# A two-layer graph kernel: the gathers of a tile issued in three parts, with a one-element GpSimd copy between them, and another order at the ends of blocks

## The chip, the core and the metric

The kernel runs on one core of a Trainium2 chip. The core has five engines that run their own instruction streams and meet only at semaphores: TensorE (PE in the profile, with its weight loads as PEld), VectorE (DVE), ScalarE (ACT), GpSimd (POOL) and SyncE (SP). Sixteen DMA engines move data between the device's memory and the on-chip memory. DMAs that take their row numbers from a list, gathers and scatters, are issued by GpSimd, which spends time on each. The metric is the device time of one execution in microseconds (us); the number to beat is the median of 12 runs.

## The reference

There are 4096 nodes with 128 features each, and an adjacency matrix of 4096 x 4096 in which about 0.8% of the entries are one, so that a node has some 32 neighbours. Two layers follow one another:

```
# layer 0: attention with 8 heads
Wh  = x @ W[h]                          # 8 heads, 128 features
e   = leaky_relu(f1[i] + f2[j], 0.2)    # f1 = Wh.a1, f2 = Wh.a2
att = softmax(e over the neighbours j of i)
h   = elu(att @ Wh);  x1 = layernorm(x + elu(concat(h) @ W1 + b1)) * gamma + beta
# layer 1: quantiles over the neighbours
keep  = neighbours of i without every m-th one (m from the number of neighbours)
agg   = mean of the 25%, 50% and 75% quantiles of x1[j], j in keep, per feature
out   = (0.5 * agg + 0.5 * x1) @ Wl.T + bl + x1
```

## The kernel before

The work goes through three stages. First, the adjacency matrix is read (ACTq line 820) and turned into lists: for each row VectorE finds the positions of the ones with maximum and replace instructions (`neighbours`, lines 811 to 870, a generator that works in small pieces). The rows of a block are then ranked by the number of their neighbours (`complete_records`, `rank_by_count`; the result is the tile `ranks`, line 998), and GpSimd scatters their records in that order to device memory (`rec_d`, line 354). There are five blocks of 4, 6, 8, 8 and 6 tiles, 128 rows each: 32 tiles in all.

Second comes the attention, tile by tile. SyncE loads the sorted records of a tile and its short lists (`load_rows`, lines 1037 to 1062). VectorE transposes them into lists of row numbers (`list_rows`: `idx`, `f1b`, `f1x`). GpSimd gathers the neighbours' rows from `xt_d` into the buffer `G` or `Gs`, 128 rows by one DMA (`fetch_rows`, through `gather`, line 345). A tile takes 27 to 49 gathers, 1152 in all. The weighing (`weigh_rows`) then works on what has landed: VectorE adds the scores (`z`, lines 1133 and 1134), ScalarE takes the exponential (line 1135), VectorE spreads it into weights (`pf`, line 1160; first half, then second half), TensorE multiplies them with the gathered rows (`y`, line 1188), ScalarE copies the product out (`raw`, line 1201), and VectorE divides by the sums: `rden` (lines 1208 and 1209), then `raw` (line 1211). Every four tiles or so, `transform` makes the layer's output from them, and its rows are scattered to `x_d` (the names `x1_d` of the source stand without digits in the profile).

Third, the quantiles: GpSimd gathers each node's kept neighbours from `x_d` (`vals`), and VectorE sorts them by comparisons (lines 1462 and 1464).

The order in the second stage is written out by hand, in one loop over tiles (lines 583 to 626). In the turn of tile k, the loop issues all gathers of tile k, and after each three of them one waiting scatter (`put_one`, line 571). Then `work(k - 1)` weighs the tile in front, whose gathers were issued in the turn before. Between the steps of the weighing stand pieces of the next block's lists (`behind`, an equal share of them, `each`, after each step), and the preparing of the next tile's row lists (`soon`). In the turn before a block's last tile, the share holds the completing and the ranking of the next block too. In the turn of the block's last tile (`end`), the scatters of the next block's records (`place(b + 1)`) go between the first gathers, and SyncE's loads of the next two tiles are issued after them. `G` has two buffers, `pf` four, `rden` two.

```
weigh.append(fetch_rows(tc, pools, ready.pop(k), xt_d, uses, put_one, k == NT - 1))
while aside:
    put_one()
if end and b < final:
    load(k + 1)
    load(k + 2)
work(k - 1, behind, left, soon)
```

Of the kernel before, what the change touches and what calls it, by code (L numbers as in the profile page):

```python
# [24 lines left out]
P = 128  # L25
# [63 lines left out]
LMAX = 2 * max(HT)  # L89
ROOM = max(2 * HT[u[0]] * len(u) for u in UNITS)  # L90
TURN = 12
EARLY = []


# [274 lines left out]
def kernel(  # L369
# [97 lines left out]

    rp = tc.alloc_tile_pool(name="recp", bufs=1)
    rec = rp.tile([P, NT, REC], F32, name="rec")
    num = rp.tile([P, NT], F32, name="num")  # L470
    oneb = rp.tile([P, P], BF16, name="oneb")
    before = rp.tile([P, P], BF16, name="before")
# [60 lines left out]
        t = sum(BLOCKS[:b]) + i  # L533
        ready[k] = list_rows(tc, pools, *loaded.pop(k), t, bad)

    def work(k, behind, quota, soon=None):

        def more():
            nonlocal quota
            if quota:  # L540
                quota -= 1
                next(behind, None)

        if k >= 0:
            R, parts = weigh.pop(0)
            at = len(members)
            members.append(R)
            each = -(-quota // (len(parts) + 9))
            for turn, _ in enumerate(
                weigh_rows(tc, attp, pp, parts, turned, at, consts, k == NT - 1)  # L550
            ):
                if soon and turn == len(parts):
                    soon()
                    soon = None
                if tails and next(tails[0], True):
                    tails.pop(0)
                for _ in range(each):
                    more()
            if len(members) == size[k]:
                tails.append(  # L560
                    transform(tc, attp, pp, kp, turned.pop(0), list(members), consts, store)
                )
                members.clear()
        if soon:
            soon()
        while quota:
            more()

    aside = []

    def put_one():
        if aside:
            scatter(nc, *aside.pop(0))

    for _ in prepare(0):
        pass
# [5 lines left out]
    with tc.manual_schedule(engines=ALL):  # L582
        for k, (b, i) in enumerate(seq):
            n = BLOCKS[b]
            end = i == n - 1
            behind, left = None, 0
            if b < final:
                if i == 0:
                    nxt = prepare(b + 1)
                    todo = BLOCKS[b + 1] * PIECES + -(-BLOCKS[b + 1] // 8) + 1  # L590
                if not end:
                    behind, left = nxt, -(-todo // (n - 1 - i))
                    todo -= left
            elif i == 0:

                cp.release()
                adjp.release()
                wp = tc.alloc_tile_pool(name="order", bufs=1, side="right")
                cp = tc.alloc_tile_pool(name="cnt_all", bufs=2, side="right", reuse_waits="tile")
                found = rank_by_count(tc, cp, kp, num, jp1, before, oneb, 0, NT)  # L600
                order = wp.tile([P, NT], I32, name="order")
                nc.vector.tensor_copy(order, found)
                cp.release()
                cp = tc.alloc_tile_pool(name="lists", bufs=2, side="right", reuse_waits="tile")
                pools.append(cp)
                waiting = list(range(NT))
            if not end:
                if i + 2 < n:
                    load(k + 2)
            soon = (lambda: prep(k + 1)) if not end else None  # L610
            aside.extend((x1_d, *args) for args in store)
            store.clear()
            if end and b < final:
                aside.extend(place(b + 1))
            if b == final:
                aside.extend((all_d, rec[:, t, 0:REC1], order[:, t : t + 1]) for t in waiting[:3])
                waiting = waiting[3:]
            weigh.append(fetch_rows(tc, pools, ready.pop(k), xt_d, uses, put_one, k == NT - 1))
            while aside:
                put_one()  # L620
            if end and b < final:
                load(k + 1)
                load(k + 2)
            work(k - 1, behind, left, soon)
            if end and b < final:
                prep(k + 1)
        for t in waiting:
            scatter(nc, all_d, rec[:, t, 0:REC1], order[:, t : t + 1])
        R = wp.tile([P, NT, REC1], F32, name="all")
        idx = wp.tile([P, NT, L], I32, name="idx")  # L630
        nc.sync.dma_start(R, all_d.rearrange("(t p) w -> p t w", p=P))
        work(NT - 1, None, 0)
        rows = kept_rows(tc, wp, R, jp1, pidx, idx, own_i, bad, limits, (0, 24, 16, 8))
        for left in range(64):
            if left == 2:
                next(rows)
            if tails and next(tails[0], True):
                tails.pop(0)
        assert not tails
        for args in store:  # L640
            scatter(nc, x1_d, *args)
        nc.vector.tensor_scalar(lane, lane, 31, None, ALU.bitwise_and)
        nc.vector.tensor_copy(lanef, lane)
        for t, parts in enumerate(every):
            for w, g in capacity(parts)[1]:
                wider = cp.tile([P, 1], F32, name="wider")
                nc.vector.tensor_scalar(wider, lanef, float(g), float(w), ALU.is_ge, ALU.mult)
                nc.vector.tensor_tensor(holds[:, t : t + 1], holds[:, t : t + 1], wider, ALU.add)
        nc.vector.tensor_tensor(bad[:, 4, :], bad[:, 4, :], holds, ALU.is_gt)
        count_bad(tc, cp, kp, bad, ones, total)  # L650
# [222 lines left out]
def complete_records(tc, cp, rec, num_all, bad, jp1, pidx, t0, n):  # L873
# [3 lines left out]
    for a in range(t0, t0 + n, step):  # L877
# [28 lines left out]
        for i, s in enumerate((sk, sk2)):  # L906
# [15 lines left out]
        nc.vector.tensor_scalar(keys, keys, -1.0, float(N), ALU.mult, ALU.add)  # L922
        nc.vector.tensor_tensor(rec.bitcast(I32)[:, a : a + m, 0:L], keys, pads, ALU.add)
        nc.vector.tensor_copy(rec[:, a : a + m, R_NUM], num)
        nc.gpsimd.iota(
            rec.bitcast(I32)[:, a : a + m, R_OWN],
            pattern=[[P, m]],
            base=a * P,
            channel_multiplier=1,
        )  # L930
        yield


# [161 lines left out]
def fetch_rows(tc, ap, lists, xt_d, turn, between, halves):  # L1095


    nc = tc.nc
    R, todo = lists
    parts = []  # L1100
    G, room = None, 0
    done = 0
    for at, (s0, w, g0, idx, f1v) in enumerate(todo):
        k = P // w
        if w - g0 > room:
            rest = 0
            for _, v, h0, _, _ in todo[at:]:
                if rest + v - h0 > 32:
                    break
                rest += v - h0  # L1110
            room = 18 if at and rest <= 18 else 32
            G, col = take(ap, [P, room, XW], "Gs" if room == 18 else "G", turn), 0
        parts.append((w, k, g0, G[:, col : col + w - g0, :], f1v))
        col += w - g0
        room -= w - g0
    for half in (0.5, 1) if halves else (1,):
        for (w, _, g0, G, _), (_, _, _, idx, _) in zip(parts, todo):
            for g in range(max(g0, int((half - 0.5) * w) if halves else 0), int(half * w)):
                gather(nc, G[:, g - g0, :], xt_d, idx[:, g : g + 1])
                done += 1  # L1120
                if done % 3 == 0:
                    between()
    return R, parts


def weigh_rows(tc, ap, pp, parts, turned, place, consts, halves):


    nc = tc.nc
# [17 lines left out]
    for half in range(2):  # L1147
        pfs = []
        for (w, k, g0, G, f1v), z in zip(parts, zs):
            g2 = w // 2  # L1150
            a = max(g0 - half * g2, 0)
            if a >= g2:
                pfs.append(None)
                continue
            if halves:
                here = slice(half * g2 + a - g0, (half + 1) * g2 - g0)
                scores(z[:, here], G[:, here, D + 1 :], f1v[:, here])
            pf = ap.tile([P, H * P // 2], F32, name="pf", bufs=4)
            spread = [P, g2 - a, k, H]
            nc.vector.tensor_tensor(  # L1160
                pf.rearrange("p (g k h) -> p g k h", g=g2, k=k)[:, a:],
                z[:, half * g2 + a - g0 : (half + 1) * g2 - g0, :].unsqueeze(2).to_broadcast(spread),
                own[w].unsqueeze(1).unsqueeze(3).to_broadcast(spread),
                ALU.mult,
            )
            pfs.append(pf)
        yield
        for b in range(4):
            if b % 2 == 0:
# [37 lines left out]
    rden = ap.tile([P, H], F32, name="rden")  # L1207
    nc.vector.tensor_scalar(rden, raw[:, :, D], TINY, None, ALU.max)
    nc.vector.reciprocal(rden, rden)
    yn = raw[:, :, 0:D]  # L1210
    nc.vector.tensor_tensor(yn, yn, rden.unsqueeze(2).to_broadcast([P, H, D]), ALU.mult)  # L1211
    yield
# [478 lines left out]
```

## Time and profile before

| what | value |
|---|---|
| median of 12 runs | 3515.74 us (3509.89 to 3520.33) |
| profiled execution | 3511.04 us |
| its span in the trace | 3509.0 us |
| busy share: DVE, POOL, ACT, PE | 75%, 65%, 36%, 22% |
| gathers of the attention: number, mean of one on GpSimd | 1004 into G, 1002 ns; 148 into Gs, 991 ns |
| gathers of the quantiles: number, mean of one | 1028, 946 ns |

The profile is of one execution; its span is 2 us shorter than that execution's time, and that is 4.7 us under the median. Busy shares are means over stages with different limits. Times inside the trace are counted from the span's start. "issue" as a releaser is time in which the engine waited for nothing that the profile shows. POOL lines of gathers and scatters show GpSimd's own part of the DMA, not the transfer.

### The profile page before, as it was taken

What the parts mean: (1) busy time and instruction counts of PE and PEld (TensorE: products, weight loads), DVE (VectorE), ACT (ScalarE), POOL (GpSimd) and SP (SyncE); (2) the same over time, 40 slices, a digit from 0 to 9 for tenths busy, and PEclk for the clock granted to TensorE, in tenths of its full rate; (3) what the DMA queues carried; (4) which work ended last, traced back from release to release, by engine and by line L of the source; (5) the groups of instructions that cost most, each with busy time, mean ns of one, the idle gap of its engine ahead of it and who ended that gap; (6) DMA issues with size and microseconds to landing.
All of it is one profiled execution on the core that took longest, in us unless ns stands there. A gap on an engine that the chain in (4) does not pass through costs nothing. (4 is left out here: it accounts for less than half of the span.)

```text
span 3509.0 us, 17209 instructions
## 1 busy us (share of the span) xinstructions
PE 758.3 (22%) x2717; PEld 439.2 (13%) x2717; DVE 2625.7 (75%) x4737; ACT 1253.1 (36%) x1843; POOL 2293.2 (65%) x2450
## 2 busy tenths in 40 slices
PE   1113524333243434234411000011000000000001
PEld 1011211211112111111300000000000000000001
DVE  7694875657545554313257999999999999999998
ACT  3132332233122312112213444444444544444443
POOL 0477777777777777777647777773575576667530
PEclk9956756666576656567655555555555555555555
DMA  5543442433333322222112122210111111112100
GB/s 186 128 135 98 126 127 68 121 107 108 78 87 107 91 55 60 59 52 52 44 39 53 53 52 53 53 52 26 37 48 38 37 49 43 43 44 52 42 22 4
DMA packets 118646, 239.35 MB, mean 68 GB/s; under 512 B 55744, under 2 KB 72128, under 8 KB 110336
## 3 DMA queue, kind: packets, MB, share of 16 engines
q0 software_dynamic: 75392, 159.16, 18.2%
q10 hardware_dynamic: 12160, 68.49, 5.7%
q1 hardware_dynamic: 30976, 10.53, 1.6%
q14 instruction: 93, 0.76, 0.1%
q8 instruction: 25, 0.41, 0.1%
HBM read 226.82 MB, written 11.18 MB: 68 GB/s over the span
## 5 line engine op out<-in xcount | busy, mean ns | idle before, releaser
L1464 DVE TENSOR_TENSOR vals<-low,vals 128x1024 f32<-128x1024 f32 (+9 forms) x1342 | 1581.3, 1215 | 64.5 <-DMA vals<-x_d,idx 22.5
L345 POOL DMA_INDIRECT vals<-x_d,idx x1028 | 972.8, 946 | 557.0 <-issue 305.7
L345 POOL DMA_INDIRECT G<-xt_d,idx x1004 | 1005.7, 1002 | 310.5 <-issue 301.7
L1462 ACT COPY low<-vals 128x1024 f32<-128x1024 f32 (+6 forms) x739 | 725.8, 984 | 917.7 <-DVE vals L1464 870.3
L1188 PE MATMUL y<-G,pf 128*64 128x258 f32 (+1 forms) x1072 | 244.6, 522 | 656.9 <-DVE pf L1160 488.4
L715 PE MATMUL fin<-share,vals 128*128 128x128 f32 x294 | 70.9, 420 | 1302.1 <-DVE vals L1464 1097.8
L1201 ACT COPY raw<-y 32x258 f32<-32x258 f32 (+1 forms) x480 | 175.0, 365 | 335.6 <-PE y L1188 331.1
L1133 DVE TENSOR_TENSOR z<-G,f1x 128x256 f32<-128x256 f32 (+6 forms) x43 | 20.4, 475 | 324.2 <-DMA G<-xt_d,idx 319.7
L715 PEld LDWEIGHTS fin<-share,vals 128*128 128x128 f32 x294 | 63.8, 317 | 1309.0 <-DVE vals L1464 1026.5
L1135 ACT ACTIVATE z<-z 128x256 f32<-128x256 f32 (+8 forms) x77 | 22.9, 302 | 548.7 <-DVE z L1134 536.0
L1188 PEld LDWEIGHTS y<-G,pf 128*64 128x64 f32 (+1 forms) x1072 | 119.5, 189 | 771.7 <-DVE pf L1160 539.7
L854 DVE MAX8 first<-sgn 128x8 f32<-128x128 bf16 x1024 | 211.9, 277 | 2.0
L345 POOL DMA_INDIRECT Gs<-xt_d,idx x148 | 146.7, 991 | 45.1 <-issue 41.8
L826 ACT ACTIVATE sgn<-adj_t 128x2048 bf16<-128x2048 int32 x64 | 122.0, 1906 | 113.1 <-DVE first L854 96.8
L1188 PE MATMUL y<-Gs,pf 128*128 128x258 f32 (+1 forms) x364 | 136.1, 485 | 0.0
L1220 ACT COPY yT<-turned 128x512 f32<-128x512 f32 x64 | 65.2, 1019 | 169.7 <-PE turned L1219 169.7
L866 DVE MAX8 rec<-first 128x8 f32<-128x256 f32 x256 | 108.8, 425 | 7.1
L354 POOL DMA_INDIRECT rec_d<-rec,ranks x32 | 33.3, 1041 | 120.1 <-DVE ranks L998 101.4
L1160 DVE TENSOR_TENSOR pf<-z,own 128x512 f32<-128x512 f32 (+2 forms) x134 | 80.2, 636 | 32.8 <-ACT z L1135 18.3
L354 POOL DMA_INDIRECT out_dram<-o,own_i x32 | 31.7, 992 | 101.1 <-ACT o L745 83.8
L1248 PE MATMUL o<-hv,W_sb 128*128 128x512 f32 (+2 forms) x160 | 80.9, 612 | 70.7 <-DVE hv L1242 70.6
L1219 PE MATMUL turned<-ident,raw 128*128 128x128 f32 x256 | 62.4, 390 | 153.6 <-DVE raw L1211 98.7
(185 smaller groups left out, 1486.5 us busy)
## 6 DMA issues: line engine op xcount, KB each, us to landing
adj_t<-in_adj_dram ACTq DMA_DIRECT2D x64, 1024.0 KB
vals<-x_d,idx POOLq DMA_INDIRECT x1028, 2.5
G<-xt_d,idx POOLq DMA_INDIRECT x1004, 2.6
R<-rec_d SPq DMA_DIRECT2D x128, 26.4 KB
score<-rec_d SPq DMA_DIRECT2D x184, 1.0 KB
Gs<-xt_d,idx POOLq DMA_INDIRECT x148, 2.6
xt_d<-rec SPq DMA_DIRECT2D x4, 548.0 KB
rec<-in_x_dram SPq DMA_DIRECT2D x4, 512.0 KB
```

Of the source, the lines that this page charges most:

```text
L345: nc.gpsimd.indirect_dma_start(out=dst, out_offset=None, in_=rows, in_offset=bass.IndirectOffsetOnAxis(ap=idx, axis=0),)
L715: nc.tensor.matmul(fin[:, i, :], lhsT=v, rhs=w, start=(a == 0), stop=(a == len(terms) - 1), skip_group_check=True,)
L826: nc.scalar.activation(sgn, adj_t, AF.Sign, accum_out=cnt[:, i : i + 1])
L854: nc.vector.max(first[:, ts(c0 // CW + c, 8)], key[:, b * (512 // CW) + c, :])
L866: nc.vector.max(top, first)
L1160: nc.vector.tensor_tensor(pf.rearrange("p (g k h) -> p g k h", g=g2, k=k)[:, a:], z[:, half * g2 + a - g0 : (half + 1) * g2 - g0, :].unsqu ...
L1188: nc.tensor.matmul(yv[p0 : p0 + m], lhsT=pf, rhs=rhs, start=not any(over[:i]), stop=not any(over[i + 1 :]), skip_group_check=True,)
L1201: nc.scalar.copy(raw[p0 : p0 + m, 4 * half + b - 1 : 4 * half + b + 1, :], y[p0 : p0 + m, :, a : a + D + 1],)
L1220: nc.scalar.copy(yT[:, :, ts(place, P)].rearrange("p h (u g) -> p g u h", u=4)[:, ts(half, 16)], t_ps.rearrange("p b (g u h) -> p (b g) u ...
L1248: nc.tensor.matmul(o, lhsT=consts["W1_sb"][:, h, :], rhs=hv[:, ts(j, n)], start=(h == 0), stop=(h == H - 1),)
L1462: nc.scalar.copy(kept, low)
L1464: nc.vector.tensor_tensor(high if end else low, kept, high, ALU.max if end else ALU.min)
```

## The change

Six edits, of which the first three make one whole:

- `fetch_rows` no longer issues the gathers. It returns a generator that stops before the 11th and before the 26th gather of the tile (`FOLLOW = (10, 25)`).
- The loop issues the first ten gathers of tile k and then calls `work(k - 1)`. When the weighing of tile k - 1 has written its first `pf`, GpSimd copies one element of that `pf` to a 1 x 1 tile `follow`, and issues the gathers up to the 25th. When the weighing has written `rden`, GpSimd copies one element of it and issues the rest. The first and the last tile's gathers are issued in one go, as before. This makes 61 copies: 31 of `pf`, 30 of `rden`, each behind a wait for VectorE.
- Since a later write to a `pf` or `rden` buffer has to wait for the copy that reads it, VectorE gets waits for GpSimd, 30 more than before.
- In the turn before a block's last tile, the completing and the ranking of the next block (`held`) come after the whole weighing, and no more between its steps. The share `each` is counted without them.
- In the turn of a block's last tile, the scatters of the next block's records start after 15 gathers in place of 3 (`later` lets four turns of `put_one` pass). SyncE's loads of the next two tiles still come behind them.
- The numbers of the own rows (`iota` into `rec`, line 925), written per block by five GpSimd instructions of which four stand between gathers, are written once at the start for all tiles.

The instructions of SyncE keep their order. On ScalarE and TensorE a few instructions of the turns before a block's last tile change places with VectorE's.

```diff
+FOLLOW = (10, 25)
...
+nc.gpsimd.iota(
+    rec.bitcast(I32)[:, :, R_OWN], pattern=[[P, NT]], base=0, channel_multiplier=1
+)
...
-    def work(k, behind, quota, soon=None):
+    def work(k, behind, quota, soon=None, held=0, issue=None, go_on=None):
...
-            if quota:
+            if quota > held:
...
-            each = -(-quota // (len(parts) + 9))
+            each = -(-(quota - held) // (len(parts) + 9))
+            seen = []
...
+                if issue and seen:
+                    nc.gpsimd.tensor_copy(follow, seen.pop()[0:1, 0:1])
+                    if next(issue, True):
+                        issue = None
+                        go_on()
...
     def put_one():
         if aside:
             scatter(nc, *aside.pop(0))
+        elif later:
+            if later[0]:
+                later[0] -= 1
+            else:
+                scatter(nc, *later[1].pop(0))
+                if not later[1]:
+                    later.clear()
...
+                    held = 0 if todo else -(-BLOCKS[b + 1] // 8) + 1
...
-                aside.extend(place(b + 1))
+                later.extend((4, place(b + 1)))
...
-            weigh.append(fetch_rows(tc, pools, ready.pop(k), xt_d, uses, put_one, k == NT - 1))
-            while aside:
-                put_one()
-            if end and b < final:
-                load(k + 1)
-                load(k + 2)
-            work(k - 1, behind, left, soon)
+            fetched, issue = fetch_rows(tc, pools, ready.pop(k), xt_d, uses, put_one, k == NT - 1)
+            weigh.append(fetched)
+            def go_on():
+                while aside or later:
+                    put_one()
+                if end and b < final:
+                    load(k + 1)
+                    load(k + 2)
+            if k == 0 or k == NT - 1:
+                for _ in issue:
+                    pass
+            else:
+                next(issue)
+            work(k - 1, behind, left, soon, held, issue, go_on)
...
-        nc.gpsimd.iota(
-            rec.bitcast(I32)[:, a : a + m, R_OWN], ...
-        )
...
+    def issue():
+        done = 0
+        for half in (0.5, 1) if halves else (1,):
+            for (w, _, g0, G, _), (_, _, _, idx, _) in zip(parts, todo):
+                for g in range(...):
+                    if done in FOLLOW:
+                        yield
+                    gather(nc, G[:, g - g0, :], xt_d, idx[:, g : g + 1])
+                    done += 1
+                    if done % 3 == 0:
+                        between()
...
+        if half == 0:
+            seen.append(pfs[0])
         yield
...
     nc.vector.reciprocal(rden, rden)
+    seen.append(rden)
```

More of the change, by code (lines that the diff above doesn't have):

```diff
@@ L547, in work @@
             members.append(R)
-            each = -(-quota // (len(parts) + 9))
+            each = -(-(quota - held) // (len(parts) + 9))
+            seen = []
             for turn, _ in enumerate(
-                weigh_rows(tc, attp, pp, parts, turned, at, consts, k == NT - 1)
+                weigh_rows(tc, attp, pp, parts, turned, at, consts, k == NT - 1, seen)
             ):
+                if issue and seen:
[3 more added lines that the diff above has]
+                        go_on()
                 if soon and turn == len(parts):
@@ L563, in work @@
                 members.clear()
+        if issue:
+            for _ in issue:
+                pass
+            go_on()
         if soon:
             soon()
+        held = 0
         while quota:
             more()
-    aside = []
+    follow = const.tile([1, 1], F32, name="follow")
+    aside, later = [], []
     def put_one():
@@ L585 @@
             end = i == n - 1
-            behind, left = None, 0
+            behind, left, held = None, 0, 0
             if b < final:
@@ L617 @@
                 waiting = waiting[3:]
-            weigh.append(fetch_rows(tc, pools, ready.pop(k), xt_d, uses, put_one, k == NT - 1))
-            while aside:
-                put_one()
-            if end and b < final:
-                load(k + 1)
-                load(k + 2)
-            work(k - 1, behind, left, soon)
+            fetched, issue = fetch_rows(tc, pools, ready.pop(k), xt_d, uses, put_one, k == NT - 1)
[7 more added lines that the diff above has]
+            if k == 0 or k == NT - 1:
+                for _ in issue:
+                    pass
+            else:
+                next(issue)
+            work(k - 1, behind, left, soon, held, issue, go_on)
             if end and b < final:
@@ L924, in complete_records @@
         nc.vector.tensor_copy(rec[:, a : a + m, R_NUM], num)
[L925 to L929, printed above, removed]
-        )
         yield
@@ L1101, in fetch_rows @@
     G, room = None, 0
-    done = 0
     for at, (s0, w, g0, idx, f1v) in enumerate(todo):
@@ L1115, in fetch_rows, with weigh_rows @@
         room -= w - g0
[L1116 to L1126, printed above, removed]
+    def issue():
+        done = 0
+        for half in (0.5, 1) if halves else (1,):
+            for (w, _, g0, G, _), (_, _, _, idx, _) in zip(parts, todo):
+                for g in range(max(g0, int((half - 0.5) * w) if halves else 0), int(half * w)):
+                    if done in FOLLOW:
[4 more added lines that the diff above has]
+                        between()
+    return (R, parts), issue()
+def weigh_rows(tc, ap, pp, parts, turned, place, consts, halves, seen):
     nc = tc.nc
```

## The prediction

> **What bounds the kernel now.** I read the page first: its engine lines and the slices, to see which engine is full in which stage.
>
> ```profile
> PE 758.3 (22%) x2717; PEld 439.2 (13%) x2717; DVE 2625.7 (75%) x4737; ACT 1253.1 (36%) x1843; POOL 2293.2 (65%) x2450
> ...
> DVE  7694875657545554313257999999999999999998
> POOL 0477777777777777777647777773575576667530
> ```
>
> A slice is 87.7 us. From slice 21 on VectorE is at 9 of 10: the quantile stage is VectorE's. In slices 3 to 20 VectorE falls to 5 and less while GpSimd stands at an even 7. The chain of waits that ended last is no help (it ends in the last scatter at once), so I asked for busy time by stage, cut where GpSimd issues its first and its last gather of the attention:
>
> ```profile
> core 0: us, PE busy (x) PEld busy (x) DVE busy (x) ACT busy (x) POOL busy (x), PEclk, DMA share, GB/s
> 126.00:1732.00 1606.00, 573.95 (x1993) 283.90 (x1993) 888.98 (x2821) 423.86 (x814) 1229.45 (x1231) 0.65 0.34 90
> ```
>
> GpSimd is busy for 1229 of 1606 us, and the waits in that window say where the other 376 are:
>
> ```profile
> POOL G L345 <- issue: 301.7, 992, 0.3
> POOL Gs L345 <- issue: 41.8, 137, 0.3
> POOL rec_d L354 <- issue: 11.4, 28, 2.2
> ...
> POOL G L345 <- DVE f1b L1082: 5.4, 1, 5.4
> ```
>
> Nearly all of it is 0.3 us before each of some 1230 DMAs, which nothing outside GpSimd causes. Its stream is one DMA after another at 1.25 to 1.3 us, and no row says that a gather waited for TensorE to free G. So this stage is GpSimd's stream, end to end, and whatever is put into it moves the end one for one: the 73 us of scatters and tails behind it and the 1704 us of quantiles follow in order. VectorE, at 889 of 1606 us, is late only where GpSimd is made to wait for it, and that is what the change does.
>
> **A copy between two gathers.** The trace of before has no GpSimd copy, but it has four small GpSimd operations between gathers, the iotas of line 925. Here is one in the timeline (start, duration, idle time before it in brackets):
>
> ```profile
> 956.89 0.94 POOL L345 DMA_INDIRECT Gs<-xt_d,idx  x1 [0.30 <-issue]
> 957.85 0.16 POOL L925 IOTA rec<- 128x8 int32 x1
> 958.16 0.95 POOL L345 DMA_INDIRECT G<-xt_d,idx  x1 [0.15 <-issue]
> 959.42 0.94 POOL L345 DMA_INDIRECT G<-xt_d,idx  x1 [0.30 <-issue]
> ```
>
> From the end of one gather to the start of the next are 957.83 to 958.16 = 0.33 us in place of 0.30: the iota lies in the 0.3 us that GpSimd needs anyway. A copy whose wait is over costs 0.02 us if it is like that. From above I bound it by 0.3 us: about the longest small operation of the start, where the affine select over 128x128 takes 0.28, with none of it hidden. I take 0.05, near the iota, which is the nearest row in place and size. For 61 copies: 3 us, ends 1 and 18. Two rows of this case plead for the upper part: a copy reads on-chip memory where the iota only writes, and gathers, which read their list there, show a mean of 1002 ns where most take 944. That is (1002 - 944) x 1004 + (991 - 944) x 148 = 65 us of lengthening over the stage, 0.06 us for each, and they lengthen mostly while VectorE runs operations with two tiles as inputs.
>
> The Trainium skill, SBUF — State Buffer, section "Who interferes with whom", says more sharply that a VectorE instruction with two SBUF inputs and a GpSimd one that reads SBUF exclude each other, whichever starts second being held for the whole of the other. By that rule, taken for the stalled copies below, each `rden` copy would be held by line 1211, the division right behind `rden`; with 1.2 us from the trace's row for it, four stalls would cost an estimated 5 us more, and the sum below would be 18. The trace has no GpSimd compute instruction beside line 1211 to show it, and my sum leaves it out.
>
> **The waits.** A wait costs what is left of the weighing of tile k - 1 when GpSimd arrives. For each turn I set the end of the first `pf` and of `rden` of tile k - 1 against the end of the 10th and of the 25th gather of tile k, all read from the timelines. The first `pf` ends 2 to 12 us after the turn's first gather starts, the 10th gather 12 to 20: no `pf` copy waits; the smallest margin is 1.2 us (turn 14). `rden` ends at 17 to 54, the 25th gather at 32 to 43. It is late in six turns: 1 by 2.7, 2 by 21.5, 5 by 6.1, 10 by 0.8, 14 by 2.8, 16 by 12.6 us. Turn 5, for one:
>
> ```profile
> 367.22 0.94 POOL L345 DMA_INDIRECT G<-xt_d,idx  x1 [0.30 <-issue]
> ...
> 400.05 0.94 POOL L345 DMA_INDIRECT G<-xt_d,idx  x1 [0.30 <-issue]
> ...
> 406.88 0.20 DVE L1209 RECIPROCAL rden<-rden 128x8 f32<-128x8 f32 x1
> ```
>
> The first row is the turn's first gather, the second its 25th, done at 400.99; `rden` is done at 407.08.
>
> Turns 2 and 16 are turns before a block's last tile, and the new order mends them. In turn 2 completing and ranking run on VectorE from 37.7 to 53.8 us and `rden` directly after; with `held` behind the weighing, and two pieces after a step in place of three, `rden` comes at about 30, before the 25th gather at 32.6. In turn 16 they run from 21.9 to 40.5; without them, and with one piece for two, `rden` comes at about 27 against 32.8. So both cost nothing; if that cover failed they would cost the 34 us above. The other four remain: 2.7 + 6.1 + 0.8 + 2.8 = 12.4 us. After a release GpSimd starts 0.26 us later (a scatter released at 1780.40 starts at 1780.66), then the copy at 0.16 and 0.15 to the next gather: 0.57 in place of 0.3, so four times 0.27 = 1.1 us more. Behind the waiting copy stand the tile's remaining gathers, then the next tile's; VectorE, ScalarE and TensorE wait for those, so the delay isn't won back.
>
> **The block ends.** The scatters of line 354 come 12 gathers, 15 us, later. At the end of block 0 GpSimd waited for `ranks` before:
>
> ```profile
> 266.22 1.67 POOL L354 DMA_INDIRECT rec_d<-rec,ranks  x1 [2.25 <-issue]
> ...
> 272.92 1.01 POOL L354 DMA_INDIRECT rec_d<-rec,ranks  x1 [1.24 <-issue]
> ```
>
> (`ranks` ended at 265.4.) Both go: 2.25 + 1.24 - 2 x 0.3 = 2.9 us. What is late next is the row lists: SyncE loads after the last scatter has landed, and the first `idx` of the next tile was there 9.1 to 9.4 us after that scatter was issued (blocks 0 to 2; all three lists after 15). The last scatter was at 33 to 41 us of a last turn of 70 to 74; at 45 to 56 it leaves the first `idx` at 55 to 66, still 7 us or more before the next tile's first gather. VectorE idles 15 us longer for the records there, off the path. The four iotas that leave the stream give 0.1 us, and the one at the start lies in the 101 us that GpSimd waits for the first `ranks`. SyncE's queue keeps its order.
>
> VectorE's new waits: a tile with five or more `pf` writes its fifth into the buffer that the copy reads, so it waits for GpSimd's 10th gather. Before, that write came at 9.9 us in turn 27 and the 10th gather ended at 17.0, at most 7 us late, in turns where `rden` has 12 to 21 us to spare. Nothing.
>
> **The sum.** 12.4 + 1.1 + 3 - 2.9 - 0.1 = +13.5 us on the profiled execution's 3511.0, so 3524.5; the median of the runs is 4.7 higher, which makes 3529. A measurement of this kernel can tell about 0.2% (7 us) from no change.
>
> **The rivals.** *Faster, by spacing out.* If pauses and the later scatters keep gathers out of VectorE's two-input operations, the 65 us of lengthening shrink. From a quarter of it on the sign turns: 16 of 65 pay the 13.5. Half of it gives -19, 3497. For it: the lengthened gathers come in runs beside VectorE work. Against: 55 and more of 61 copies find their wait over, so the gathers keep their places. *No difference.* The four late turns are paced by VectorE's pieces, and a delay of GpSimd in one gives VectorE air for the rest; then the waits vanish and +1 - 3 leaves about -2 to +4: 3514 to 3520. Against: VectorE waits for the gathers at the start of each weighing (320 us in total), so it starts the next one late by as much. *Slower, by a chain of waits.* If the weighing slips by 5 us against the gathers, turns with less margin join (4, 6, 8, 13, 22 and 24 have 1.0 to 4.7): 12 us from them and 20 from the four, +45, 3561. That the copies don't hold GpSimd at all is excluded: each carries a wait for VectorE, and the gathers behind it are in the same stream.
>
> **How the numbers follow.** The forecast (+5 to +30) has 0.55, the chain 0.12, no difference 0.13, faster by spacing 0.20. Of the forecast's share 0.05 lies under +7. So faster 0.20, same 0.18, slower 0.62. The forecast's own range is 3518 to 3546. For 8 in 10 I go down to 3504, which takes in no difference and the weak half of spacing out, and up to 3548: copies at their upper end with the four waits are 12.4 + 1.1 + 18 - 3 = +28.5, 3544, and a little of the chain.
>
> **What would show it.** Right: copies at 0.1 to 0.2 us in some 0.3 us of gap; GpSimd's waits for `rden` in turns 1, 5, 10 and 14 and 12 us in all; none for `pf`; the two waits for `ranks` gone; the last attention gather some 13 us later; gathers' means at 1002 and 991. Wrong: a mean of G gathers under 985 (spacing out); `rden` waits in ten or more turns (chain); none at all (no difference); a gather waiting for `idx` at a block's end, for which I have priced nothing.

## The result, and the profile after

The changed kernel takes 3551.4 us (median of 7 runs, 3545.8 to 3554.5) against 3515.7 before (28 runs): a ratio of 1.0101, 95% interval 1.0091 to 1.0110, so 32 to 39 us slower. Its profiled execution spans 3547.8 us, 38.8 more than the one before. On another occasion the same kernel took 3550.3 against 3513.3, ratio 1.0105 (1.0090 to 1.0121). The profiled execution of before lies 4.7 us under its median and this one 1.8, so the difference between the profiled executions is some 3 us larger than that of the medians.

I read the same views again. The engine lines of the page, and the stretch from the first to the last gather of the attention:

```profile
PE 753.9 (21%) x2717; PEld 438.0 (12%) x2717; DVE 2624.9 (74%) x4737; ACT 1253.3 (35%) x1843; POOL 2314.4 (65%) x2507
```

```profile
core 0: us, PE busy (x) PEld busy (x) DVE busy (x) ACT busy (x) POOL busy (x), PEclk, DMA share, GB/s
125.90:1770.20 1644.30, 567.89 (x1991) 282.19 (x1991) 886.98 (x2817) 423.81 (x813) 1250.32 (x1287) 0.65 0.33 88
```

The stretch is 1644 us long where it was 1605 (the window of before above ends 0.7 us behind its last gather), and that is the whole difference: what lies ahead of the first and behind the last gather is unchanged. VectorE has nearly the same work in it, 887 us where it was 889. GpSimd is busy 21 us more, and idle 18 us more; these are rows of its waits, from the start to 1850 us:

```profile
POOL follow L558 <- DVE rden L1243: 14.9, 4, 7.5
...
POOL all_d L355 <- issue: 12.8, 18, 7.8
...
POOL rec_d L355 <- issue: 8.5, 28, 0.3
...
POOL follow L558 <- DVE pf L1192: 6.5, 2, 4.9
```

The columns are total, number and longest. Four copies wait for `rden` and two for `pf`. The first scatter into all_d, which had 0.3 us ahead of it, now has 7.8. The two waits for `ranks` at the end of block 0 are gone (28 scatters at 0.3 each). And this is the price of the copies themselves, from the view by groups (x count, busy, mean ns, idle before):

```profile
L558 POOL COPY follow<-rden 1x1 f32<-1x1 f32 x30 | 10.2, 340 | 15.0 <-DVE rden L1243 14.9
L558 POOL COPY follow<-pf 1x1 f32<-1x1 f32 x31 | 9.8, 318 | 6.6 <-DVE pf L1192 6.5
```

For the 60 copies inside the stretch: 19.9 us of busy time, and 9.5 us in place of 18.3 from them to the next DMA, so 11.1 us net. The stream's books close: waits for `rden` 14.9, for `pf` 6.5, the copies 11.1, the scatter into all_d 7.5, the waits for `ranks` -2.9, and 1.9 from all that remains (G gathers at a mean of 1005 ns, Gs at 975), together 39.

### The profile page after: what moved, and what is told of

Same layout as the page of the kernel before. It is cut to its first block, busy times and chain, and to the rows that moved or that the text cites. A ratio compares the mean times of both kernels' runs of the same rounds, so it can differ in the third digit from the quotient of the medians.

```text
span 3547.8 us, 17318 instructions
## 1 busy us (share of the span) xinstructions
PE 753.9 (21%) x2717; PEld 438.0 (12%) x2717; DVE 2624.9 (74%) x4737; ACT 1253.3 (35%) x1843; POOL 2314.4 (65%) x2507
## 5 line engine op out<-in xcount | busy, mean ns | idle before, releaser
L346 POOL DMA_INDIRECT G<-xt_d,idx x1004 | 1009.0, 1005 | 302.4 <-issue 286.1
L1167 ACT ACTIVATE z<-z 128x256 f32<-128x256 f32 (+8 forms) x77 | 23.0, 302 | 645.7 <-DVE z L1166 645.3
L1192 DVE TENSOR_TENSOR pf<-z,own 128x512 f32<-128x512 f32 (+2 forms) x134 | 80.2, 635 | 37.9 <-POOL follow L558 21.5
L1095 DVE COPY bad<-R 128x1 f32<-128x1 f32 x32 | 4.7, 148 | 132.3 <-DMA R<-rec_d 132.3
```

The lines of the kernel that those rows point to most:

```text
L346: nc.gpsimd.indirect_dma_start(out=dst, out_offset=None, in_=rows, in_offset=bass.IndirectOffsetOnAxis(ap=idx, axis=0),)
L1192: nc.vector.tensor_tensor(pf.rearrange("p (g k h) -> p g k h", g=g2, k=k)[:, a:], z[:, half * g2 + a - g0 : (half + 1) * g2 - g0, :].unsqu ...
```

## Where the waits come from: the block ends

Turn 5 looks as predicted, only longer: the first row is the turn's 25th gather, the others what GpSimd and VectorE do about the copy.

```profile
402.84 0.94 POOL L346 DMA_INDIRECT G<-xt_d,idx  x1 [0.30 <-issue]
411.24 1.17 POOL L558 COPY follow<-rden 1x1 f32<-1x1 f32 x1 [7.46 <-DVE rden L1243]
```

```profile
410.90 0.20 DVE L1243 RECIPROCAL rden<-rden 128x8 f32<-128x8 f32 x1
411.14 1.23 DVE L1246 TENSOR_TENSOR raw<-raw,rden 128x1024 f32<-128x1024 f32 x1
```

The copy is released with `rden`, comes to lie beside the division of line 1246, and takes 1.17 us. The four copies that waited for `rden` all took 1.16 or 1.17.

The waits for `pf` stand in turns 5 and 10, 1.6 and 4.9 us. Turn 10 is the first turn behind the end of block 1 (turn 5 is the second behind that of block 0), and the reason stands in VectorE's timeline before it:

```profile
598.63 0.17 DVE L1242 TENSOR_SCALAR rden<-raw 128x8 f32<-128x8 f32 x1 [2.11 <-ACT raw L1235]
...
635.51 0.15 DVE L1095 COPY bad<-R 128x1 f32<-128x1 f32 x1 [34.02 <-DMA R<-rec_d]
...
645.53 0.45 DVE L1114 STREAM_TRANSPOSE f1x<-f1b 128x256 f32<-128x256 f32 x1
645.90 0.60 DVE L1165 TENSOR_TENSOR z<-G,f1x 128x256 f32<-128x256 f32 x1
```

The same place in the trace of before, where turn 10 began at 633.0:

```profile
607.03 0.15 DVE L1068 COPY bad<-R 128x1 f32<-128x1 f32 x1 [17.30 <-DMA R<-rec_d]
...
616.89 0.45 DVE L1087 STREAM_TRANSPOSE f1x<-f1b 128x256 f32<-128x256 f32 x1
617.26 0.60 DVE L1133 TENSOR_TENSOR z<-G,f1x 128x256 f32<-128x256 f32 x1
```

VectorE waits 34 us for the records of the next block, where it waited 17; over the stage its waits for them are 132.3 us in six, where they were 70.2. Turn 10 begins at 645.7. Before, the lists (`f1x` is the last of them) were complete 16 us ahead of that turn and VectorE had begun the weighing (`z`) by then; now they are complete as it starts. So the first `pf` ends at 18.5 us of the turn, not at 10, and `rden` at 43.5, not at 35.5.

The same at the last block's end. There VectorE has, behind the lists, the ranking of all 32 tiles, which ends with `order`; the scatters into all_d need it:

```profile
1463.08 0.18 DVE L626 COPY order<-ranks 128x32 int32<-128x32 int32 x1
1463.45 0.60 DVE L1165 TENSOR_TENSOR z<-G,f1x 128x256 f32<-128x256 f32 x1 [0.19 <-issue]
1464.03 1.00 POOL L355 DMA_INDIRECT all_d<-rec,order  x1 [7.80 <-issue]
```

The same in the trace of before:

```profile
1415.78 0.18 DVE L602 COPY order<-ranks 128x32 int32<-128x32 int32 x1
...
1424.92 1.00 POOL L354 DMA_INDIRECT all_d<-rec,order  x1 [0.30 <-issue]
```

`order` was complete at 1416.0 there and the first of these scatters was issued at 1424.9, so it waited for nothing. In the changed kernel the wait is labelled "issue", but the scatter reads `order`, and starts 0.8 us after its end.

That gives the theory: the late block ends cost the 7.5 us, all of the `pf` waits and part of the `rden` waits; the copies cost 11 us, because VectorE's two-input operations hold them; what is left are the four late turns that the prediction priced. The rival: the copies and their waits make all of it.

## Experiments

**The scatters where they were.** Copies and `held` stay.

```diff
-                later.extend((4, place(b + 1)))
+                later.extend((0, place(b + 1)))
```

> The copies and `held` stay; the next block's records are scattered again right behind the third gather of a block's last tile. Theory (late records): the scatters that come 15 us later keep VectorE idle for the records (132.3 us in 6 waits against 70.2 before), so that the next block's lists, the weighing and `order` stand 15 us later in its queue. Then this run loses the 7.8 us wait ahead of the first scatter into all_d in turn 26 and both `pf` waits (6.5 us), its `rden` waits fall from 14.9 to about 12, near the 12.4 of the prediction, and the waits for `ranks` at the end of block 0 come back (2.9 us): 38.9 - 7.5 - 6.5 - 2.5 + 2.9 = +25 us over before, some 3541. Rival (the copies by themselves): the `pf` waits and the late `order` come from VectorE being held by copies and waits earlier in the stream, the ends have no part in it, and only the 2.9 come back: +42 us, some 3557, with all_d still waiting 7 us or more.

Measured: 3536.7 us against 3516.5, ratio 1.0058 (1.0043 to 1.0074), so +20 us (15 to 26), where the theory expected 25 and the rival 42; the profiled execution, 3537.5, has a stretch of 1630.2 us, 25 more than before. GpSimd's waits:

```profile
POOL rec_d L355 <- DVE ranks L1025: 104.0, 2, 101.3
...
POOL follow L558 <- DVE rden L1243: 11.2, 4, 5.0
...
POOL all_d L355 <- issue: 5.7, 19, 0.3
```

No wait for `pf`, none ahead of all_d, a wait of 2.8 us for `ranks` back, and the `rden` waits at 1.5, 5.0, 1.5 and 3.4 us in turns 1, 5, 10 and 14. That is the theory, and the 11.2 us stand close to the prediction's 12.4, which were worked out for these ends. Some 15 of the 36 us between the medians belong to the later scatters.

**The new order without copies.** All gathers of a tile in one go; `held` and the later scatters stay.

```diff
-            if k == 0 or k == NT - 1:
-                for _ in issue:
-                    pass
-            else:
-                next(issue)
-            work(k - 1, behind, left, soon, held, issue, go_on)
+            for _ in issue:
+                pass
+            go_on()
+            work(k - 1, behind, left, soon, held)
```

> The new order at the block ends (`held`, scatters 12 gathers later) stays; the gathers of a tile are issued in one go and there is no copy. Theory: what is left is the late `order` in turn 26 (+7.5 us) and the gone waits for `ranks` (-2.9): +3 to +7 us, 3519 to 3523, with VectorE's waits for the records still near 130 us in 6, and no wait of GpSimd for `pf` or `rden`. Rival (the order alone makes the weighing late enough to stop the gathers, by G buffers that come free too late): +15 us or more, with waits of G for TensorE or VectorE in the stream. Second rival (`order` is late only because the copies delayed VectorE): -3 us, 3513, and no wait ahead of the first scatter into all_d.

Measured: 3516.6 against 3516.5, ratio 1.0002 (0.9993 to 1.0011). The late `order` is there without any copy, which rules out the second rival:

```profile
POOL all_d L355 <- issue: 13.3, 19, 7.8
```

VectorE's waits for the records are 128.3 us in six, and no gather waits for a buffer. But the time came in lower than expected: the interval ends at +4 us. The stretch of the profiled execution is 4.5 us longer than before, at which the books stand (7.5 - 2.9), while the medians are equal: the profiled execution of before lies 4.7 us under its median, this one 0.4. So whether the 5 us are paid isn't settled; by itself the new order costs 4 us at most. It becomes dear with copies, since only they make GpSimd wait for the late weighing of turns 5 and 10.

**Copies that need not wait.** 61 copies at the same places, of a constant.

```diff
-                    nc.gpsimd.tensor_copy(follow, seen.pop()[0:1, 0:1])
+                    seen.pop()
+                    nc.gpsimd.tensor_copy(follow, ones[0:1, 0:1])
```

> 61 copies at the same places in the stream, of one element of a constant that was written at the start, in place of `pf` and `rden`: they read as before but wait for nothing. Theory (a copy costs by what VectorE does beside it): the copies still come to a mean of some 250 to 320 ns, since most of them meet VectorE's two-input operations by chance, the four that stood right beside line 1246 lose their 1.17 us; all 21.4 us of waits are gone, and the late `order` stays: 5 to 9 + 7.5 - 2.9 = +10 to +14 us, some 3527. Rival (the lengthening comes from the wait's release, which puts the copy beside the next VectorE operation): all copies at 177 ns, 61 x 0.03 = 2 us, so +7 us, some 3522.

**The same, but writing only.**

```diff
-                    nc.gpsimd.tensor_copy(follow, seen.pop()[0:1, 0:1])
+                    seen.pop()
+                    nc.gpsimd.memset(follow, 0.0)
```

> 61 memsets of the one element at the same places, which write and read nothing, and wait for nothing. Theory (a GpSimd operation that reads on-chip memory is what VectorE's two-input operations hold): none is lengthened, all lie near the 0.16 us of the iotas or the 0.18 of a free copy, and this run is 3 to 7 us faster than the one with ready copies: about +6 us over before, some 3521. Rival (any small GpSimd operation is held, writing ones too): the same mean and the same spread up to 0.5 us and more as the ready copies, and the same time within 2 us.

Measured: ready copies 3530.3 us, ratio 1.0036 (1.0025 to 1.0047); memsets 3518.6, ratio 1.0010 (1.0001 to 1.0019), both against 3516.5. Operations of `follow` in the one and the other (shortest, median and longest in ns):

```profile
L559 POOL COPY follow<-ones x61: 177/177/1217, 181.1 to 1752.2; 1x1 f32<-1x1 f32 x61
```

```profile
L559 POOL MEMSET follow<- x61: 88/88/339, 179.9 to 1738.4; 1x1 f32 x61
```

Three quarters of the copies take 177 or 178 ns, which adds 0.03 us to the stream, near the prediction's 0.05. 15 of 61 take over 200, each of them beside a VectorE operation with two tiles as inputs or beside the scaling `e<-e`; the mean is 264. The rule has exceptions: four copies of 177 or 178 ns touch such an operation as well (three of the operations began after the copy, the fourth, `hv<-key,e`, reads a tile that TensorE wrote), and five lie beside MATCH_REPLACE8, which names two tiles too. The same place in turn 6 of both kernels, here of the copy:

```profile
444.29 1.23 DVE L1247 TENSOR_TENSOR raw<-raw,rden 128x1024 f32<-128x1024 f32 x1
444.33 1.22 POOL L559 COPY follow<-ones 1x1 f32<-1x1 f32 x1
...
445.71 0.97 POOL L346 DMA_INDIRECT G<-xt_d,idx  x1 [0.16 <-issue]
```

and here of the memset:

```profile
439.39 1.22 DVE L1247 TENSOR_TENSOR raw<-raw,rden 128x1024 f32<-128x1024 f32 x1
439.43 0.09 POOL L559 MEMSET follow<- 1x1 f32 x1
...
439.74 1.69 POOL L346 DMA_INDIRECT G<-xt_d,idx  x1 [0.22 <-issue]
```

The memset passes through the division; the gather behind it, which reads its list, takes 1.69 us. In the copy's case the copy has waited already, and the gather takes 0.97, as it does behind most copies (0.94 elsewhere). Twelve memsets lie so beside a two-input operation at 88 or 89 ns. The four that were lengthened most, to 282 to 339 ns, all stand beside the scaling of line 1276, `e<-e`, which has one tile as input; a fifth, of 152 ns, stands beside the copy `f1b<-score`. Two more memsets beside `e<-e` took 88 and 89 ns; there the scaling began after the memset.

The Trainium skill, SBUF — State Buffer, section "Who interferes with whom", says that a two-input VectorE operation contends with a GpSimd instruction that reads SBUF and not with one that only writes it, and that scalings can enter a mode in which VectorE takes the shared port pair for reading and writing. Both halves agree with these rows: the copy at 1.22 against the memset at 0.09 us, and the memset at 0.34 beside `e<-e`. That it is the ports that hold them, no row shows.

In the stream the ready copies cost 7.2 us net, the memsets 0.2; the medians differ by 12 us, of which 5 more are G gathers that ran longer in the kernel with copies (1009 ns against 1004; why, these runs don't show). The theory's +10 to +14 held for the copies. The memsets came to +2, some 4 us under the +6 expected, as the kernel without copies did; between the profiled executions it is +7.

**Only the last end as before, and no `held`.** Two edits of the changed kernel, each alone, and beside them a candidate for the better of both: no copies, and the scatters later at the end of block 0 alone, by 6 gathers.

```diff
-                later.extend((4, place(b + 1)))
+                later.extend((4 if b + 1 < final else 0, place(b + 1)))
```

```diff
-                    held = 0 if todo else -(-BLOCKS[b + 1] // 8) + 1
+                    held = 0
```

```diff
-                later.extend((4, place(b + 1)))
+                later.extend((2 if b == 0 else 0, place(b + 1)))
```

What was expected, in this order:

> As the changed kernel, but the records of the last block alone are scattered again right behind the third gather. Theory: the 7.8 us wait ahead of the first scatter into all_d in turn 26 goes, since VectorE then ends `order` before that turn; everything ahead of turn 25 stays as it is: -7.5 us, some 3544. Rival (`order` is late by the delays piled up in VectorE over the whole stage): the wait stays above 5 us and the time within 2 us of the changed kernel.

> As the changed kernel, but with `held` at 0: completing and ranking of the next block run again between the steps of the weighing in turns 2 and 16. Theory: `rden` comes at about 54 us of turn 2 and at about 45 of turn 16, so the `rden` copies wait there for some 20 and 12 us: +30 us over the changed kernel, some 3581. Rival (the delay in those turns is won back, since VectorE does the same work in either order): the waits appear but later ones shrink by as much, +0 to +10 us, 3551 to 3561.

> No copies, `held` kept; only at the end of block 0 do the scatters come later, and by 2 between-places (6 gathers, 7.5 us) in place of 4; at the other ends they stand where they stood before. Theory: the two waits for `ranks` at the end of block 0 shrink or go (ranks ended at 265.4, the first scatter was issued at 266.2), nothing else is late: -2 to -3 us, 3513, at the edge of what can be measured. Rival (the reordering of VectorE's pieces by `held` alone costs time in turns 2 and 16): +2 us or more.

These three were first measured on an occasion when the kernel before itself took 3996.5 us; the ratios there were 1.0121 (1.0064 to 1.0178), 1.0252 (1.0195 to 1.0309) and 1.0006 (0.9978 to 1.0034). They say little on the expectations, whose times go by a kernel before of 3516 us, and are taken up under the hardware below. All three were measured again, with the changed kernel beside them. The expectations put the 3997 us down to the chip, but the record has the same chip number, 6, for both occasions, so that isn't shown.

> The changed kernel with the records of the last block alone scattered right behind the third gather again, on a chip like that of the kernel before. Theory: only the 7.8 us wait ahead of the first scatter into all_d goes, -7.5 us against the changed kernel, 3544; the `pf` waits of turns 5 and 10 stay at 6 us. Rival (`order` is late by what piled up in VectorE ahead): the wait stays above 5 us and the time within 2 us of the changed kernel.

> The changed kernel with `held` at 0, measured again on a chip where the kernel before takes its 3516 us (on the chip of the first look the kernel before itself took 3997). Theory: `rden` waits of some 20 us in turn 2 and some 12 in turn 16 come on top: +30 us over the changed kernel, some 3581. Rival (the delay is won back, VectorE does the same work in either order): later waits shrink by as much, +0 to +10 us, 3551 to 3561.

> No copies, `held` kept, scatters later at the end of block 0 alone and by 6 gathers in place of 12, on a chip like that of the kernel before. Theory: the waits for `ranks` at that end go and nothing else is late: -2 to -3 us, some 3513, at the edge of what can be measured. Rival (`held` alone makes VectorE later in turns 2 and 16): +2 us or more.

> The changed kernel as it is, for the comparison on one chip: 3551 us, and in its trace 15 us of `rden` waits in four turns, 6.5 us of `pf` waits in two and 7.8 us ahead of the first scatter into all_d. If the `pf` waits are an accident of one execution they are gone in this one; if they come from the block ends they stand in turns 5 and 10 again.

Measured against 3513.3: the changed kernel 3550.3; with the last end as before 3543.2 (ratio 1.0082, 1.0067 to 1.0097); without `held` 3583.9 (1.0201, 1.0186 to 1.0217); the candidate 3512.3 (0.9995, 0.9986 to 1.0004).

With the last end as before the wait ahead of all_d is gone and the other two are what they were, to the tenth:

```profile
POOL follow L558 <- DVE rden L1243: 14.9, 4, 7.5
...
POOL follow L558 <- DVE pf L1192: 6.5, 2, 4.9
POOL all_d L355 <- issue: 5.6, 19, 0.3
```

The median is 7.1 us less than the changed kernel's, 7.5 expected: `order` was late by the last block's records and by nothing else. Without `held`:

```profile
POOL follow L558 <- DVE rden L1243: 48.0, 6, 21.5
...
POOL follow L558 <- DVE pf L1192: 4.9, 1, 4.9
```

Two more waits, 21.5 us in turn 2 and 12.4 in turn 16, and 33.6 us more in the median. The prediction priced that cover at 21.5 and 12.6 from the trace of before, and little of it is won back: turn 5 waits 1.6 us less for `pf` and 1.3 less for `rden`. The repeated changed kernel shows its `pf` waits of 1.6 and 4.9 us in turns 5 and 10 again, so they are no accident. The candidate can't be told from the kernel before: no version measured here beats it.

## Why the prediction was right and wrong

*The bound: right.* GpSimd's stream sets the end of the stage, and what is put into it moves the end one for one: 39.0 us in the stream, 38.8 in the span. The direction and the mechanism, GpSimd held by the weighing of the tile in front, are those of the forecast.

*The size: wrong*, +13.5 forecast and +38.8 measured in the profiled executions (+36 between the medians). Term by term:

- The copies, 3 us taken and 18 as upper end; 11.1 measured. The value for a free copy was right (0.03 us where the iota's row had given 0.02). Wrong was to take the iota, which reads nothing, as the nearest row for all 61. The prediction had the objection in its hands, the gathers lengthened beside two-input operations, and kept it for the range alone. The rule of the Trainium skill (SBUF — State Buffer, "Who interferes with whom"), which it left out of the sum, was right on the four stalled `rden` copies: four times 1.0 us over a free one, 4 of the 8 us missed here. The rest are copies that met such an operation by chance or behind `pf`.
- The `rden` waits, 12.4 and 1.1 for the restart; 14.9 measured, restart included. The turns were the four named. With the scatters in their old place it would have been 11.2.
- The `pf` waits, none; 6.5 measured. "No `pf` copy waits" was read from the turns of before, whose first `pf` the change moves in turn 10 by 8 us.
- The block ends, -2.9. The waits for `ranks` did go. The failed step is "VectorE idles 15 us longer for the records there, off the path". The margin that was checked was that of the gathers for `idx`, and it held: no gather waited. But behind the lists in VectorE's stream, which stood still for 34 us until the records came, stood the weighing, which the change had just made GpSimd wait for, and at the last end the ranking that ends with `order`. The idle time that the prediction put at nothing was on the path. That is the 7.5 us ahead of all_d, all of the `pf` waits and some 4 us of the `rden` waits (14.9 against 11.2).
- `held`: right, and shown by taking it away (33.6 us, 34 priced). VectorE's new waits for the copy, 21.5 us in three, cost nothing that the sum shows: right, though the longest is 11.2 us and not "at most 7".
- Two small slips changed nothing: the forecast's +5 is 3521 on the medians, where its range begins at 3518; and "33 to 41 us" for the last scatter leaves out the last block's, which stood at 29.

*The rivals.* Faster by spacing out is out: G gathers 1005 ns on average, not under 985. No difference is out: the waits stand. The chain is out in its own form, `rden` is waited for in four turns and not in ten or more, but its premise came true in one place: where the weighing slipped by 8 us, in turn 10, both copies of the turn were late. It came from the block end and not from the piling up of delays: with the scatters where they were, the `pf` wait of that turn is gone and its `rden` wait is 1.5 us in place of 3.3.

## What to carry to other kernels

When a change delays one step, follow every instruction that stands behind its consumer in the same engine's stream, not only the transfer it feeds; and set the margins of one edit against the times that the other edits leave, not against those of before. What a small operation on GpSimd cost here went by what it reads and by what VectorE ran at that moment: 61 memsets came to 0.2 us in the stream, a copy of one element took anything from 0.18 to 1.2 us. Where a wait is put in front of an instruction that becomes ready together with a two-input VectorE operation, add the length of that operation to the price.

## What the runs showed of the hardware

- A GpSimd copy of one element takes 0.177 us between two DMAs and a memset 0.088, and they leave 0.16 and 0.21 us to the next DMA in place of 0.30: 0.03 us for a free copy, nothing for the memset. The gather behind a free copy took 0.97 us in place of 0.94, another 0.03.
- On the occasion when the kernel before took 3996.5 us, VectorE stood still inside chains that otherwise ran nearly without a gap. The group of line 899 in the kernel with the last end as before, first on that occasion and then on the later one:

```profile
L899 DVE MAX8 rec<-first 128x8 f32<-128x256 f32 x224 | 95.7, 427 | 85.6 <-remote 62.3 <-DVE first L901 11.3 <-issue 5.4
```

```profile
L899 DVE MAX8 rec<-first 128x8 f32<-128x256 f32 x224 | 95.7, 427 | 7.0
```

The same 427 ns each, but 85.6 us of idle time in front in place of 7.0. With VectorE late everywhere, GpSimd waited for `rden` in 26 turns and 330 us, yet the kernel was only 1.2% slower than the one before on that occasion. There the gathers wait without copies as well: in the candidate 243 us for TensorE to free G. What holds VectorE up there wasn't found out.
